# Softmax sums by row reductions instead of matmuls, in the first attention block of a four-block kernel

## The chip, the cores and the metric

The kernel runs on one core of one Trainium2 chip. The metric is the time on the device in microseconds (us). The core has five engines that run beside one another, each in the order of its own list of instructions: TensorE (PE; its weight loads are shown as PEld), VectorE (DVE), ScalarE (ACT), GpSimd (POOL) and SyncE (SP, which only issues DMAs here). They wait for each other through semaphores. PE writes to PSUM, which has 8 banks; DVE and ACT read the results from there.

## The reference

Four blocks follow one another on rows of 256 features. Only the first one is changed: a transformer block on x of shape (2, 2048, 256) with 16 query heads and 4 key heads of 16 features, a causal window of 64 keys, and a feed-forward part of 1024 features. Cut to what matters:

```python
h = layernorm(x, g1, b1)                       # applied to an already normalised x, see below
q, k, v = h @ Wq + bq, h @ Wk + bk, h @ Wv + bv
q, k = rope(q), rope(k)                        # 4 query heads share a key head
scores = q @ k.T / sqrt(16)
valid = (col <= row) & (row - col < 64)
attn = softmax(where(valid, scores, -1e9))     # exp(s - max) / sum(exp(s - max))
out = attn @ v
x = x + out @ Wo + bo
h2 = layernorm(x, g2, b2)
x = x + gelu(h2 @ Wf1 + bf1) @ Wf2 + bf2
```

Each block of the chain is preceded by a layer normalisation, so the kernel handles the first two normalisations of x together ("normalised twice" and "normalised once" in the code). After the first block come two layers of local attention with a gated feed-forward part, a gated attention block and a ternary linear layer. All data is float32.

## The kernel before, in words

**Tiles.** The 4096 rows of the first block are 32 tiles of 128 rows (the index t), in 8 groups of 4 tiles (the index g). A tile goes through a pipeline of four steps: in step t its queries, keys and values are computed, in step t+1 its scores, in step t+2 it attends, and in step t+3 the output projection is added. So a step works on four tiles at once, named in `step_a` p (project), q (scores), a (attend) and o (output). Layer normalisation and the feed-forward part (FFN) work on whole groups and are spread over the steps. Steps run from −5 to 35; the steps' numbers modulo 4 tell what a step holds besides its tiles: types 0 and 1 hold four of the eight FFN hidden products each (L555, two at each of two places in the step, `fill(0)` and `fill(1)`; each is two matmuls and one GELU, L561), types 2 and 3 hold FFN output products (L566, added by L573). Type 2 ends with the normalisation and transposes of the next group (`m`), type 3 with those of the FFN input (`f`).

**What a tile does, by line.** `project` (L383) makes a 128x384 product for queries, keys and values. `take` adds the bias (L392, DVE), copies the values to `vo` (L395, POOL) with one or two DMAs that shift half of the rows into `vmid`, and forms the two parts of the rotation: t2 on POOL (L406, L409), t1 on DVE (L414). `rotate` adds them (L419, L424, DVE) into a padded layout. `to_features` transposes that on PE (L430, L431), and ACT copies it out (L436, L437, L439). In the next step `scores` makes the products (L449) in 4 banks, `mask(g)` adds the mask for one key head (L459, DVE), `maxima(half)` takes row maxima over 128 keys for 8 heads (L468, DVE) and subtracts them (L469, POOL), and `exponents` (L472, ACT) takes the exponential of all 16 heads. In the step after that, `weights_to_keys` transposes the weights on PE (L479) and ACT copies them out (L487). `values` multiplies them with the values (L499), and once more with a matrix of ones (`one48`, L506), which gives each softmax sum, repeated over the 16 features of its head, in the second half of the same bank. `take_values` takes its reciprocal (L515, DVE, 128x256 elements from PSUM) and multiplies (L516). `output` (L521) and its addition to the residual (L527, DVE) come a step later.

**Normalisation.** The statistics are made on DVE and POOL (L145, L146, L162 or L135 and L137). `normalised_twice` (L169) and `normalised` (L197) apply them to four tiles on DVE; `normalised_once` (L178, L183) does it on ACT for the residual rows. `transposed` (L214 on PE, L219 on ACT) brings the result into features. `add_rows` (L206, POOL) adds biases and residuals.

**Order.** The lists of PE, DVE, ACT and POOL are in the order in which `step_a` calls these functions (the program is scheduled by hand); the SP queue's DMAs are ordered by a scheduler. Tiles of SBUF come from pools with a tag and a number of buffers, PSUM banks from one pool of 8. The call order within a step before the change is: scores, masks 0 and 1, project, take, mask 2, rotate, maxima 0, mask 3, maxima 1; fill 0; statistics; to_features; weights_to_keys and take_weights (ahead of to_features in steps without FFN work); fill 1; normalise; values and take_values; output and add_output; exponents; the groups' transposes; bias.

Of the kernel before, what the change touches and what calls it, by code (L numbers as in the profile page):

```python
# [17 lines left out]
P = 128  # L18
# [3 lines left out]
GT = 4  # L22
# [23 lines left out]
def kernel(ctx: ExitStack, tc: tile.TileContext, I: dict, out: bass.AP):  # L46
# [118 lines left out]
    def normalised_twice(src, stats, dst):  # L165

        mv, rs = stats
        for t in range(GT):
            nc.vector.tensor_scalar(  # L169
                dst[:, t, :], src[:, t, :], mv[:, t, 0:1], rs[:, 1, t : t + 1], ALU.subtract, ALU.mult  # L170
            )

    def normalised_once(src, stats, dst, residual):

        mv, rs = stats
        scale = rs[:, 0, :]
        shift = T(small, [P, GT], "sh2")
        nc.vector.scalar_tensor_tensor(shift, mv[:, :, 0], -1.0, scale, ALU.mult, ALU.mult)  # L178
        if residual:
            scale = T(small, [P, GT], "sc2")  # L180
            nc.vector.tensor_scalar_add(scale, rs[:, 0, :], 1.0)
        for t in range(GT):
            nc.scalar.activation(  # L183
                dst[:, t, :], src[:, t, :], AF.Identity,
                bias=shift[:, t : t + 1], scale=scale[:, t : t + 1],
            )
# [91 lines left out]
    class GroupA:  # L278
# [9 lines left out]

        def normalise(self):
            self.h = T(wa, [P, GT, D], "h", 1)  # L290
            normalised_twice(self.xg, self.stats, self.h)

        def residual(self):
            self.y = T(wa, [P, GT, D], f"y{self.g % 3}", 1)
# [74 lines left out]
    nc.gpsimd.memset(one48, 0.0)  # L369
    nc.gpsimd.memset(one48[:, AHD : 2 * AHD], 1.0)  # L370

    class TileA:


        def __init__(self, t, grp):
            self.t, self.grp = t, grp
            self.first = t % TPS == 0

        def project(self):
            hT, tt = self.grp.hT, self.t % GT  # L380
# [8 lines left out]
        def take(self):  # L389
            t, tl = self.t, self.t % TPS  # L390
            qkv = self.qkv = T(wa, [P, 384], "qkv")
            nc.vector.tensor_add(qkv, self.pm[:, :384], bqkvA)  # L392

            vo = vown[t % NVW]
            nc.gpsimd.tensor_copy(  # L395
                vo[:, :, AHD : 2 * AHD], qkv[:, 320:384].rearrange("p (g d) -> p g d", d=AHD)
            )
            load(vmid[t % NVW][64:128], vo[0:64])
            if tl < TPS - 1:
                load(vmid[(t + 1) % NVW][0:64], vo[64:128])  # L400

            nh, hf = AH + AKV, AHD // 2
            qk = self.qk = qkv[:, 0:320].rearrange("p (h d) -> p h d", d=AHD)
            sin = ropeA[:, tl, 1, :].unsqueeze(1)
            t2 = self.t2 = T(wa, [P, nh, AHD], "t2")
            nc.gpsimd.tensor_mul(  # L406
                t2[:, :, 0:hf], qk[:, :, hf:AHD], sin[:, :, 0:hf].to_broadcast([P, nh, hf])
            )
            nc.gpsimd.tensor_mul(  # L409
                t2[:, :, hf:AHD], qk[:, :, 0:hf], sin[:, :, hf:AHD].to_broadcast([P, nh, hf])  # L410
            )
            cos = ropeA[:, tl, 0, :].unsqueeze(1)
            self.t1 = T(wa, [P, nh, AHD], "t1", 1)
            nc.vector.tensor_mul(self.t1, qk, cos.to_broadcast([P, nh, AHD]))  # L414

        def rotate(self):
            nh, t1, t2 = AH + AKV, self.t1, self.t2
# [53 lines left out]
        def exponents(self):  # L471
            nc.scalar.activation(self.S, self.S, AF.Exp, scale=1.0 / AHD**0.5)  # L472

        def weights_to_keys(self):
            self.pts = []
            for g in range(AKV):
                pt = bank4()
                for c in range(AG):
                    nc.tensor.transpose(pt[:, c, :], self.S[:, g * AG + c, :], ident)  # L479
                self.pts.append(pt)  # L480
# [9 lines left out]
        def values(self):  # L490

            pm = self.po = bank().rearrange("p (s k q) -> p s k q", s=2, k=2)
            vw = (vmid[self.t % NVW], vown[self.t % NVW])
            for b in range(2):
                q = slice(64 * b, 64 * b + 64)
                for e in range(2):
                    c0 = 0 if e else AHD
                    for g in range(AKV):
                        nc.tensor.matmul(  # L499
                            pm[32 * g : 32 * g + 32, 0, :, q], vw[b][:, g, c0 : c0 + 32],  # L500
                            self.PT[g // 2][:, g % 2, :, e, q], start=e == 0, stop=e == 1,
                        )
            for e in range(2):
                c0 = 0 if e else AHD
                for g in range(AKV):
                    nc.tensor.matmul(  # L506
                        pm[32 * g : 32 * g + 32, 1, :, :], one48[:, c0 : c0 + 32],
                        self.PT[g // 2][:, g % 2, :, e, :], start=e == 0, stop=e == 1,
                    )

        def take_values(self):
            pm = self.po
            self.oT = T(wa, [P, KC, P], "oT")
            rd = T(wa, [P, KC, P], "rdA", 1)
            nc.vector.reciprocal(rd, pm[:, 1])  # L515
            nc.vector.tensor_mul(self.oT, pm[:, 0], rd)  # L516

        def output(self):
            pm = self.pm = bank()
# [9 lines left out]
    class FfnA:  # L529
# [9 lines left out]

        def normalise(self):  # L540
            self.h = T(wa, [P, GT, D], "h", 1)
            normalised(self.y, self.stats, self.h)
            add_rows(self.y, lambda t: bf2)

            add_rows(self.xr, lambda t: self.y[:, t, :])
# [43 lines left out]
        steps.setdefault(step, {}).setdefault(what, []).append(args)  # L589

    for t in range(NT):
        at(t, "project", t)
        at(t + 1, "scores", t)
        at(t + 2, "attend", t)
        at(t + 3, "output", t)
# [19 lines left out]
    def step_a(todo):  # L615
        p = a = q = o = n = m = f = e = None
        for (g,) in todo.get("load", ()):
            if g:
                groups_a[g] = GroupA(g)
        if "project" in todo:  # L620
            (t,) = todo["project"][0]
            if t == GT:
                weights.update({**load_qkv(0), **load_wo(0), **load_ffn(0)})
            p = tiles_a[t] = TileA(t, groups_a[t // GT])
        if "scores" in todo:
            q = tiles_a[todo["scores"][0][0]]
        if "attend" in todo:
            a = tiles_a[todo["attend"][0][0]]
        if "output" in todo:
            o = tiles_a.pop(todo["output"][0][0])  # L630
        for (g,) in todo.get("residual", ()):
            ffns_a[g] = FfnA(groups_a[g])
        if "statistics" in todo:
            n = groups_a[todo["statistics"][0][0]]
        if "normalise" in todo:
            m = groups_a[todo["normalise"][0][0]]
        if "prepare" in todo:
            f = ffns_a[todo["prepare"][0][0]]
        if "finish" in todo:
            e = ffns_a.pop(todo["finish"][0][0])  # L640

        def fill(place):

            rest = []
            for g, what, i in todo.get(f"fill{place}", ()):
                x = ffns_a[g]
                if what == "hidden":
                    rest.append(lambda x=x, i=i, r=x.hidden(i): x.take_hidden(i, r))
                else:
                    rest.append(lambda x=x, i=i, r=x.output(i): x.take_output(i, r))  # L650
            return rest

        if q:
            q.scores()
            q.mask(0)
            q.mask(1)
        if p:
            p.project()
            p.take()
        if q:  # L660
            q.mask(2)
        if p:
            p.rotate()
        if q:
            q.maxima(0)
            q.mask(3)
            q.maxima(1)
        pieces = fill(0)
        if a and not pieces:
            a.weights_to_keys()  # L670
            a.take_weights()
        for r in pieces:
            r()
        if n:
            n.statistics()
        if f:
            f.statistics()
        if e:
            e.last_statistics()
        if p:  # L680
            p.to_features()
            p.take_features()
        if a and pieces:
            a.weights_to_keys()
            a.take_weights()
        for r in fill(1):
            r()
        if m:
            m.normalise()
        if f:  # L690
            f.normalise()
        if e:
            e.last_normalise()
        if a:
            a.values()
            a.take_values()
        if o:
            o.output()
            o.add_output()
        if q:  # L700
            q.exponents()
        if m:
            m.to_features()
            m.residual()
        if f:
            f.to_features()
        for (g,) in todo.get("bias", ()):
            groups_a[g].add_bias()

# [1013 lines left out]
```

## Time and profile before

| | us |
|---|---|
| time, median of 3 runs | 2645.26 (2644.18 to 2648.4) |
| profiled execution, its own time | 2644.28 |
| its span in the profile | 2642.5 |
| first block, start to about | 500 |

The profile is of one execution. Busy times are sums for an engine or a group of instructions, "idle before" is what the engine waited just ahead of the group and for whom. Of the first block, these groups matter here (all from the groups by line for the first 680 us; xcount is the number of instructions):

| line, engine | what | xcount | mean ns |
|---|---|---|---|
| L506 PE | ones times weights, the sums | 512 | 387 |
| L499 PE | values times weights | 1024 | 283 |
| L430 PE | transposes of queries | 128 | 284 |
| L515 DVE | reciprocal of the sums, 128x256 | 32 | 1752 |
| L468 DVE | row maxima, 128x1024 | 64 | 1215 |
| L459 DVE | masks, 128x512 | 128 | 681 |
| L197 DVE | normalise FFN rows | 32 | 614 |
| L169 DVE | normalise rows of a group | 32 | 505 |
| L183 ACT | normalise residual rows | 32 | 592 |
| L561 ACT | GELU, 128x512 | 64 | 688 |

Each of these float32 matmuls stands in the trace as two records, so xcount and the chain's counts are twice the number of calls. Matmuls are pipelined, so the mean of one is longer than the time from one to the next: the chain of waits, which counts only the time by which each moves the end, is the better source for what a group of matmuls costs.

### The profile page before, as it was taken

The page shows a single profiled execution, that of the slowest core. Times are in us where ns is not written, and L with a number is a line of the kernel's source. Part 1 is how long each engine was busy: PE and PEld are TensorE (multiplying, and loading weights), DVE is VectorE, ACT ScalarE, POOL GpSimd, SP SyncE. Part 2 cuts the span into 40 slices and gives each one's busy share as a digit, 9 for nine tenths or more (in the row PEclk, how much of TensorE's full clock was granted, in tenths as well). Part 3 has the DMA queues.
Part 4 walks back from the last instruction along what each step waited for, and adds up shares of the span by engine and source line. Part 5 has one row for each costly group of instructions (what it writes and reads, how often), then busy time and mean ns, then how long its engine had stood idle before and what let it go on. Part 6 is the DMA issues. An engine that isn't in the chain of part 4 may idle for free.

```text
span 2642.5 us, 51312 instructions
## 1 busy us (share of the span) xinstructions
PE 2576.2 (97%) x20130; PEld 1645.9 (62%) x20130; DVE 1608.4 (61%) x4357; ACT 1199.7 (45%) x2507; POOL 995.4 (38%) x1237
## 2 busy tenths in 40 slices
PE   6899999998999999999999999999999999999998
PEld 4577777666666666666676676666544455445567
DVE  6878777567666766667666667774434335434344
ACT  3555555465666666756567666663500001500000
POOL 5565555545434544435444445542200002300011
PEclk8999999999999999999999999999999999999999
DMA  5001101111001011011310111101100000100000
GB/s 171 17 31 32 32 32 40 47 33 51 25 17 26 25 26 29 22 55 29 89 37 18 29 34 37 25 22 53 40 8 4 6 7 12 44 0 6 5 11 13
DMA packets 73169, 82.03 MB, mean 31 GB/s; under 512 B 18829, under 2 KB 57056, under 8 KB 72672
## 3 DMA queue, kind: packets, MB, share of 16 engines
q1 hardware_dynamic: 72928, 78.75, 10.6%
q8 instruction: 160, 2.62, 0.4%
q14 instruction: 81, 0.66, 0.1%
HBM read 44.20 MB, written 10.50 MB: 21 GB/s over the span
## 4 chain that ended last, share of the span: by engine, by line
PE 91%; DVE 4%; POOL 3%; issue 1%; DMA 0%; ACT 0%; SPq 0%; POOLq 0%; ACTq 0%; DVEq 0%
PE ps L1576 17%; PE ps L900 12%; PE ps L1154 10%; PE ps L1177 6%; PE ps L1500 4%; PE ps L566 4%; PE ps L555 4%; PE ps L1082 4%; PE ps L975 3%; PE ps L1053 2%; PE ps L1519 2%; PE ps L1488 2%; PE ps L1025 2%; PE ps L956 2%; PE ps L1478 2%; PE ps L479 2%
## 5 line engine op out<-in xcount | busy, mean ns | idle before, releaser
L1576 PE MATMUL ps<-room 128*128 128x512 f32 (+1 forms) x1152 | 463.2, 544 | 0.0
L1576 PEld LDWEIGHTS ps<-room 128*128 128x128 f32 x1152 | 217.8, 189 | 221.9 <-issue 214.7
L900 PE MATMUL ps<-room 128*128 128x512 f32 x768 | 347.4, 602 | 0.0
L1006 ACT ACTIVATE room<-room,shift,rn 128x192 f32<-128x192 f32 x512 | 276.0, 546 | 71.7 <-DVE shift L994 71.7
L921 POOL TENSOR_TENSOR room<-room 128x256 f32<-128x256 f32 x128 | 113.5, 887 | 500.6 <-ACT room L912 500.6
L1154 PE MATMUL ps<-room 128*128 128x512 f32 x640 | 287.6, 593 | 0.4 <-ACT room L219 0.4
L1544 ACT COPY room<-ps 128x256 f32<-128x256 f32 x32 | 11.8, 370 | 587.7 <-PE ps L1542 587.7
L939 POOL TENSOR_TENSOR rn<-ss,mhalf 128x8 f32<-128x8 f32 x128 | 248.2, 1939 | 10.7
L900 PEld LDWEIGHTS ps<-room 128*128 128x128 f32 x768 | 141.0, 190 | 157.8 <-issue 149.9
L1506 DVE SCALAR_TENSOR_TENSOR room<-ps,room 128x512 f32<-128x512 f32 (+1 forms) x144 | 90.1, 626 | 206.5 <-PE ps L1500 206.5
L1154 PEld LDWEIGHTS ps<-room 128*128 128x128 f32 x640 | 118.8, 190 | 137.3 <-issue 131.5
L1529 POOL TENSOR_SCALAR veC<-mvC 128x1 f32<-128x1 f32 x32 | 7.2, 224 | 453.2 <-DVE mvC L1527 453.2
L1177 PE MATMUL ps<-room 128*128 128x256 f32 x768 | 173.0, 379 | 0.0
L987 DVE CUSTOM_DVE_ANT_0 room<-ps,room 128x192 f32<-128x192 f32 x512 | 152.2, 353 | 14.7 <-PE ps L975 14.3
L1177 PEld LDWEIGHTS ps<-room 128*128 128x128 f32 x768 | 143.7, 190 | 24.8 <-issue 6.2
L1017 DVE TENSOR_SCALAR room<-room,rdB 128x192 f32<-128x192 f32 x512 | 151.7, 360 | 4.5
L1170 DVE SCALAR_TENSOR_TENSOR room<-ps,room 128x512 f32<-128x512 f32 x96 | 72.1, 751 | 125.6 <-PE ps L1154 86.8
L469 POOL TENSOR_TENSOR room<-room,mxA 128x1024 f32<-128x1024 f32 x64 | 120.2, 1898 | 58.5 <-PE ps L431 45.4
L936 DVE TENSOR_REDUCE ss<-room 128x8 f32<-128x512 f32 x128 | 81.9, 681 | 94.9 <-ACT room L914 94.9
L1500 PE MATMUL ps<-room 128*128 128x512 f32 (+1 forms) x288 | 133.4, 545 | 0.0
L219 ACT ACTIVATE room<-ps,room 128x512 f32<-128x512 f32 x80 | 58.1, 772 | 143.3 <-PE ps L214 143.0
L1082 PE MATMUL ps<-room 128*128 128x256 f32 x512 | 121.0, 379 | 0.0
(182 smaller groups left out, 5050.1 us busy)
## 6 DMA issues: line engine op xcount, KB each, us to landing
room<-room SPq DMA_DIRECT2D x144, 128.0 KB
room<-in_L_attn_x_dram SPq DMA_DIRECT2D x16, 512.0 KB
room<-in_rope_b_dram SPq DMA_DIRECT2D x16, 512.0 KB
xs<-room SPq DMA_DIRECT2D x8, 512.0 KB
room<-xs SPq DMA_DIRECT2D x8, 512.0 KB
room<-in_rope_c_dram SPq DMA_DIRECT2D x8, 512.0 KB
out_dram<-R SPq DMA_DIRECT2D x32, 128.0 KB
room<-in_L_ffn_w_dram SPq DMA_DIRECT2D x6, 640.0 KB
```

The lines of the kernel that those rows point to most:

```text
L469: nc.gpsimd.tensor_sub(Sh, Sh, mc.unsqueeze(2).to_broadcast([P, 2 * AG, P]))
L900: nc.tensor.matmul(pm, src[:, cols], self.w["wqkv"][:, k, part * BIN : (part + 1) * BIN], start=k == 0, stop=k == 1,)
L921: nc.gpsimd.tensor_mul(u2[:, :, 0:hd2], x[:, :, hd2:BHD], sin[:, :, 0:hd2].to_broadcast([P, BH, hd2]))
L939: nc.gpsimd.tensor_tensor(self.rn[part], ss, mhalf[:, 0:BH], ALU.pow)
L987: nc.vector.tensor_tensor_reduce(S[:, e, jj, :], sc[e][:, jj * KW : (jj + 1) * KW], self.mask[:, jj, :], 1.0, -3.0e38, ALU.add, ALU.max, t ...
L1006: nc.scalar.activation(S[:, e, jj, :], S[:, e, jj, :], AF.Exp, bias=self.shift[half][:, a : a + 1], scale=self.rn[0][:, head : head + 1], ...
L1017: nc.vector.tensor_scalar_mul(S[:, e, jj, :], S[:, e, jj, :], rd[:, a : a + 1])
L1082: nc.tensor.matmul(pm[:, 0:D], self.oT[:, k, :], wo[:, k, :], start=k == 0, stop=k == BIN // P - 1)
L1154: nc.tensor.matmul(pm, w["w1"][:, k, half, c * P : (c + 1) * P], hT[:, k, :], start=k == 0, stop=k == KC - 1,)
L1177: nc.tensor.matmul(pm[:, 0:D], hh[:, c, tt * P : (tt + 1) * P], self.w["w2"][:, c, :], start=c == 0, stop=c == BNC - 1,)
L1500: nc.tensor.matmul(pm[:, 0:n], self.KT[:, J * P : (J + 1) * P], self.QT[:, q0 : q0 + n], start=True, stop=True,)
L1576: nc.tensor.matmul(acc[e][:, 0:n], self.V[:, J, e * P : (e + 1) * P], s2, start=J == 0, stop=J == TPS - 1,)
```

## The change

It has four parts.

1. From tile 6 on (`by_features` is false), the matmuls with ones (L506) and the large reciprocal (L515) are left out. In their place, `sum_weights` at the very end of the attending step takes row sums of the exponentials on DVE (two reductions of 128x1024) and the reciprocal of the 16 sums of a row. At the next step, `spread_sums` on ACT repeats each reciprocal over 16 features, `sums_to_features` transposes this on PE (two transposes) and copies it out on ACT, and `take_values` multiplies (so it comes a step later than before, just ahead of the output projection's place in the order).
2. Tiles 1 to 6 are projected one step earlier; their `take` and `rotate` come ahead of the masks and maxima (`p.t < RAMP`).
3. For group 1's first normalisation and group 0's FFN normalisation, four ACT instructions take the place of four DVE instructions (`normalised_on_scalar`).
4. In `take`, the two t2 products on POOL and t1 on DVE come ahead of the value copy and its DMAs; t2 has one buffer instead of two.

The diff, cut to its core:

```diff
+    def normalised_on_scalar(src, mean, scale, dst):
+        shift = T(small, [P, GT], "sh2")
+        nc.vector.scalar_tensor_tensor(shift, mean, -1.0, scale, ALU.mult, ALU.mult)
+        for t in range(GT):
+            nc.scalar.activation(
+                dst[:, t, :], src[:, t, :], AF.Identity,
+                bias=shift[:, t : t + 1], scale=scale[:, t : t + 1],
+            )
...
         def normalise(self):                       # GroupA; FfnA alike with self.g == 0
-            normalised_twice(self.xg, self.stats, self.h)
+            if self.g == 1:
+                mv, rs = self.stats
+                normalised_on_scalar(self.xg, mv[:, :, 0], rs[:, 1, :], self.h)
+            else:
+                normalised_twice(self.xg, self.stats, self.h)
...
+    RAMP = 7
...
+            self.by_features = t < RAMP - 1
...
+        def sum_weights(self):
+            sums = T(wa, [P, AKV * AG], "sumsA", 1)
+            for half in range(2):
+                heads = slice(half * 2 * AG, (half + 1) * 2 * AG)
+                nc.vector.reduce_sum(sums[:, heads], self.S[:, heads, :], axis=AX.X)
+            self.rd = T(wa, [P, AKV * AG], "rdA", 1)
+            nc.vector.reciprocal(
+                self.rd.rearrange("p (k g e) -> p g k e", g=AKV, k=2),
+                sums.rearrange("p (g k e) -> p g k e", g=AKV, k=2),
+            )
+        def spread_sums(self):
+            self.rx = T(wa, [P, AKV * AG, AHD], "rx", 1)
+            nc.scalar.copy(self.rx, self.rd.unsqueeze(2).to_broadcast([P, AKV * AG, AHD]))
+        def sums_to_features(self):
+            pt = bank4()
+            for k in range(2):
+                nc.tensor.transpose(pt[:, k, :], self.rx[:, 2 * AG * k : 2 * AG * (k + 1), :], ident)
+            self.rT = T(wa, [P, KC, P], "rT", 1)
+            nc.scalar.copy(self.rT, pt[:, 0:KC, :])
...
-            for e in range(2):
+            for e in range(2) if self.by_features else ():
                 c0 = 0 if e else AHD
                 for g in range(AKV):
                     nc.tensor.matmul(                      # one48, L506
...
-            rd = T(wa, [P, KC, P], "rdA", 1)
-            nc.vector.reciprocal(rd, pm[:, 1])
-            nc.vector.tensor_mul(self.oT, pm[:, 0], rd)
+            if self.by_features:
+                self.rT = T(wa, [P, KC, P], "rT", 1)
+                nc.vector.reciprocal(self.rT, pm[:, 1])
+            nc.vector.tensor_mul(self.oT, pm[:, 0], self.rT)
...
-        at(t, "project", t)
+        at(t - 1 if 0 < t < RAMP else t, "project", t)
+        at(t, "take", t)
...
         if q:
             q.scores()
-            q.mask(0)
-            q.mask(1)
-        if p:
-            p.project()
+        for (t,) in todo.get("project", ()):
+            tiles_a[t].project()
+        if p and p.t < RAMP:
             p.take()
+            if q:
+                q.mask(0)
+                q.mask(1)
+            p.rotate()
+            if q:
+                q.maxima(0)
+                q.mask(2)
+        else:
+            ...                                   # the order before, with project ahead of mask(0)
...
+        if o and not o.by_features:
+            o.spread_sums()
         if p:
             p.to_features()
             p.take_features()
+        if o and not o.by_features:
+            o.sums_to_features()
+            o.take_values()
...
         if a:
             a.values()
-            a.take_values()
+            if a.by_features:
+                a.take_values()
         if o:
             o.output()
             o.add_output()
...
         if f:
             f.to_features()
+        if a and not a.by_features:
+            a.sum_weights()
```

More of the change, by code (lines that the diff above doesn't have):

```diff
@@ L392, in take @@
             nc.vector.tensor_add(qkv, self.pm[:, :384], bqkvA)
[L394 to L400, printed above, removed]
             nh, hf = AH + AKV, AHD // 2
@@ L404, in take @@
             sin = ropeA[:, tl, 1, :].unsqueeze(1)
-            t2 = self.t2 = T(wa, [P, nh, AHD], "t2")
+            t2 = self.t2 = T(wa, [P, nh, AHD], "t2", 1)
             nc.gpsimd.tensor_mul(
@@ L414, in take @@
             nc.vector.tensor_mul(self.t1, qk, cos.to_broadcast([P, nh, AHD]))
+            vo = vown[t % NVW]
+            nc.gpsimd.tensor_copy(
+                vo[:, :, AHD : 2 * AHD], qkv[:, 320:384].rearrange("p (g d) -> p g d", d=AHD)
+            )
+            load(vmid[t % NVW][64:128], vo[0:64])
+            if tl < TPS - 1:
+                load(vmid[(t + 1) % NVW][0:64], vo[64:128])
         def rotate(self):
@@ L472, in exponents @@
             nc.scalar.activation(self.S, self.S, AF.Exp, scale=1.0 / AHD**0.5)
+        def sum_weights(self):
[7 more added lines that the diff above has]
+                sums.rearrange("p (g k e) -> p g k e", g=AKV, k=2),
+            )
+        def spread_sums(self):
[7 more added lines that the diff above has]
+            nc.scalar.copy(self.rT, pt[:, 0:KC, :])
         def weights_to_keys(self):
@@ L541, in normalise @@
             self.h = T(wa, [P, GT, D], "h", 1)
-            normalised(self.y, self.stats, self.h)
+            if self.g == 0:
+                mv, rs = self.stats
+                normalised_on_scalar(self.y, mv[:, :, 0], rs, self.h)
+            else:
+                normalised(self.y, self.stats, self.h)
             add_rows(self.y, lambda t: bf2)
@@ L619, in step_a @@
                 groups_a[g] = GroupA(g)
-        if "project" in todo:
-            (t,) = todo["project"][0]
+        for (t,) in todo.get("project", ()):
             if t == GT:
                 weights.update({**load_qkv(0), **load_wo(0), **load_ffn(0)})
-            p = tiles_a[t] = TileA(t, groups_a[t // GT])
+            tiles_a[t] = TileA(t, groups_a[t // GT])
+        if "take" in todo:
+            p = tiles_a[todo["take"][0][0]]
         if "scores" in todo:
@@ L654, in step_a @@
             q.scores()
-            q.mask(0)
-            q.mask(1)
-        if p:
-            p.project()
+        for (t,) in todo.get("project", ()):
+            tiles_a[t].project()
+        if p and p.t < RAMP:
             p.take()
-        if q:
[L661 to L665, printed above, removed]
+            if q:
[5 more added lines that the diff above has]
+                q.mask(2)
+        else:
+            if q:
+                q.mask(0)
+                q.mask(1)
+            if p:
+                p.take()
+            if q:
+                q.mask(2)
+            if p:
+                p.rotate()
+            if q:
+                q.maxima(0)
+        if q:
             q.mask(3)
```

## The prediction

> **What bounds the kernel now.** I read the page's shares, its slices, the windows of the first block, the chain of waits in a steady stretch, then single instructions around the edit. On the page:
>
> ```profile
> PE 2576.2 (97%) x20130; PEld 1645.9 (62%) x20130; DVE 1608.4 (61%) x4357; ACT 1199.7 (45%) x2507; POOL 995.4 (38%) x1237
> ```
>
> PE is busy for 97% of the span, so only what shortens PE's own list, or an idle stretch of PE, can move the end. The windows (columns PE, PEld, DVE, ACT, POOL busy, clock, DMA) show where such stretches are in the first block:
>
> ```profile
> 40.00:60.00 20.00, 16.74 (x274) 11.84 (x275) 19.22 (x29) 10.78 (x18) 9.90 (x10) 0.91 0.80 226
> ...
> 260.00:340.00 80.00, 80.00 (x875) 59.52 (x874) 62.17 (x123) 42.35 (x66) 40.83 (x46) 1.00 0.11 34
> ```
>
> Until about 105 us DVE is nearly full (19.22 of 20 us) and PE waits for it; from 120 to 500 us PE has no gap. One steady step, as the chain of waits has it (start, length):
>
> ```profile
> 302.82 1.06 PE ps L521 x4
> 303.89 1.14 PE ps L449 x63
> 305.02 1.49 PE ps L383 x4
> 306.51 3.43 PE ps L555 x8
> 309.94 0.44 PE ps L430 x4
> 310.38 0.11 PE ps L431
> 310.49 1.75 PE ps L479 x16
> 312.24 3.44 PE ps L555 x8
> 315.67 1.01 PE ps L499 x32
> 316.68 0.86 PE ps L506 x16
> 317.55 1.06 PE ps L521 x4
> ```
>
> The step is 14.72 us (L521 to L521); steps with the second FFN product (L566) and one L214 are 15.64 us apart on average. L506 is what the change removes. From the starts in the timeline (316.50 for L506, 317.48 for L521, with the overlap of neighbouring groups that the chain cuts off) it holds PE for 0.97 us.
>
> **The change, part by part.**
>
> *Sums on PE.* 26 tiles (6 to 31) lose L506: 26 × 0.97 = 25.2 us. They gain two transposes at L430's rate (0.44/4 = 0.11 us each): 26 × 0.22 = 5.7 us. Gross: −19.5 us, −0.75 per tile, if nothing waits.
>
> *Sums on DVE.* The groups (busy, mean ns):
>
> ```profile
> L468 DVE TENSOR_REDUCE mxA<-room 128x8 f32<-128x1024 f32 x64 | 77.8, 1215 | 1.1
> ...
> L515 DVE RECIPROCAL room<-ps 128x256 f32<-128x256 f32 x32 | 56.1, 1752 | 39.4 <-PE ps L506 39.4
> ...
> L1544 ACT COPY room<-ps 128x256 f32<-128x256 f32 x32 | 11.8, 370 | 587.7 <-PE ps L1542 587.7
> ```
>
> Two row sums of L468's shape stand against one L515. [...] By the rows here, a sum costs 1.215 us for 1024 elements, and the reciprocal 1.752 us for 256. A sum of this shape isn't in the trace, but the second block has one of 512 elements (L936, 681 ns), so it lies between 1.215 (L468's maximum of the same shape) and 1.36 (two of L936); I take L468's, 1.13 from start to start. The reciprocal of 16 numbers lies between L1014 (168 ns for 4) and half of L515; I take 0.24. So DVE goes from 1.75 to 2.5 us per tile. [...] By the rows DVE goes from 62.2 to about 62.2 + 5 × 0.75 = 66 of 80 us, so it isn't full and PE keeps the saving, less what the place costs: the 2.5 us stand at the end of a step, ahead of the next tile's masks.
>
> *Waits that this makes,* each per step (types are the step's number modulo 4):
> - Steps of type 2 (FFN product, no L214 before them). With P the start of L383: the residual sum L527 runs at P−1.02, the row sums and reciprocal fill DVE to P+1.85, where the masks L459 used to start at P+0.41. Two masks bring L392 to P+3.04, the rotation L419 to P+4.69 (t2 now precedes the copy L395 on POOL, else 0.45 later), L430 to P+5.26. PE gets there at P+4.85 (319.67 to 324.52 in the trace). Wait 0.41, plus 0.13 in the later weight transposes for the fourth mask's bank: 0.54.
> - Types 0 and 1 (hidden products L555). ACT's new copy of the reciprocals (bounds L437's 275 and L436's 585 ns; L1544's 0.37 taken, same size) stands behind the step's second GELU:
>
> ```profile
> 295.06 0.60 PE L430 MATMUL ps<-ident,room 128*128 128x128 f32 x4
> ...
> 295.26 0.69 ACT L561 ACTIVATE room<-ps,room 128x512 f32<-128x512 f32 x1 [1.03 <-PE ps L555]
> ...
> 295.85 0.58 ACT L436 COPY room<-ps 128x512 f32<-128x512 f32 x1
> ```
>
>  That GELU starts 0.20 after L430; 0.59 later the copy, 0.37 later its end, with hand-over 1.21 after L430's start. PE wants it 0.55 after: 0.66 us of wait. L436 to L439, the new rT copy (0.37) and L487 queue behind it on ACT; L499, which needs L487, has 2.3 us in hand (282.97 against 285.29), so nothing more is lost. The rotation's lateness of 0.41 passes inside the 0.66.
> - Type 3 (f.normalise, L197): PE arrives at its L214 0.97 earlier. In the trace L197 runs from 285.84 to 288.05 and L214 starts at 288.13; the first three transposes need only the first three rows, so they can precede the last row by 3 × 0.11, and L214 can come 0.40 earlier, not 0.97. Wait 0.57.
>
> Net per step −0.09, −0.09, −0.21, −0.18: −0.57 per four. Steps 9 to 31: 23/4 × 0.57 = −3.3 us. Step 8 has no transposes yet: −0.97. Steps 32 to 34 have no feature transposes between GELU and sum transposes, so PE meets the wait whole (1.21): +0.46, +0.46, and +0.22 in step 34: +1.1.
>
> If waits of this size lowered PE's clock, they'd cost far more; from 60 to 80 us PE had 1.82 us of idle in small pieces and the granted clock was 1.00, so I charge nothing.
>
> *The ramp* (0 to 105 us). Projection a step ahead frees L392 from PE, but in step 1 DVE waits for group 1's x, landing at 31.47, and in step 2 for POOL, whose rs and bias rows (L162, L206) hold the rotation until 39.7, nearly as before (39.93). Rows on ACT take L169 (2.95 us) off DVE, and put 4 × 0.515 us on ACT ahead of the exponentials L472 and the copies L219, so that project(4), now in step 3, waits for L219 until about 49.4: the reciprocal of step 3 comes at +0.2. Steps 4 and 5 then win 0.5 each, the masks no longer waiting for L383; the FFN rows of group 0 on ACT end near 103.8 instead of 104.66. I take −0.95 (bounds: −4, L169 and part of L197's 2.2 kept whole; +3, ACT's two row blocks in PE's way).
>
> *At nothing:* L395 and two vmid DMAs moved behind t2 on POOL and SP (1.03 us later; their reader L499 is two steps away, 25 us; without that cover 1.0 per step); t2 with one buffer (its reader is the same step's L419); L516 moved (same 0.42); the output bank held a step longer (seven of eight banks are otherwise free in turn; the one wait found is the 0.13).
>
> Sum: −3.3 − 0.97 + 1.1 − 0.95 = −4.1 us. The profiled execution is 2644.28 us, 1.0 under the median of 2645.26; the median becomes 2641.2.
>
> **Rivals.**
> - *The waits are mostly absent.* For it: DVE has slack inside a step (2.95 us idle before L515 at 317.62), and PE's arrival times could shift by more than the waits. Then −19.5 − 1 ≈ 2625; half of the waits gone, 2633. Against: gelu order and DVE order are fixed, and the times above come from starts in the trace.
> - *DVE's lateness binds (slower).* Place: masks and rotation behind the row sums. Each 0.1 us more there delays L430 in about three of four steps: 23 × 0.75 × 0.1 = 1.7 us. From 0.25 us per tile on (a row sum of 1.34 instead of 1.215) the 4.1 are gone; at 0.55 (1.49 each) it's +9.5 − 4.1, 2650.7. For it: the 1.85 us shift is larger than any slack before L430. Against: L468 varies little.
> - *ACT rows delay the ramp:* +3 instead of −0.95, 2645.
>
> **How the numbers follow.** About 0.2% (5.3 us) is what a measurement of this kernel tells from no change, and the forecast's −4.1 lies just inside. The forecast with its own bounds (−10 to 0, so 2635 to 2645): 48%, of it 0.20 beyond −5.3. Waits absent: 21%, all faster. DVE binds: 24%, of it 0.20 past +5.3. Ramp: 7%, of it 0.02 past +5.3. So faster 0.20 + 0.21 = 0.41, slower 0.20 + 0.02 = 0.22, same the remaining 0.37. Range: the forecast, most of the first rival (to 2630) and of the second (to 2651).
>
> **What would show it.** Right: in the profile after, from 120 to 490 us PE idles about 14 us, waiting at the first sum transpose for the ACT copy by 0.6 to 0.7 in steps with L555 and at L430 for DVE by 0.4 in others; L506 has 96 entries left; step pitch 14.6. Wrong: PE without gaps (first rival), or gaps above 1 us before L430 (second). A clock under 1.00 in those windows, or a ramp that ends more than 3 us off 105, would also break the sum.

## The result, and the profile after

The changed kernel is slower: 2655.24 us (median of 6 runs, 2652.62 to 2656.69) against 2644.5 us (6 runs of the kernel before beside it), a ratio of 1.0037 with a 95% interval of 1.0024 to 1.005. I had forecast 2641.2 in a range of 2630 to 2651. The profiled execution took 2654.86 us, its span is 2653.1 against 2642.5.

Line numbers from here on are those of the changed kernel, where they have moved: scores L468, projection L402, bias L411, t2 L417 and L420, value copy L428, rotation L438 and L443, query transposes L449, masks L478, maxima L487, row sums L498, their reciprocal L501, its copy L508, sum transposes L513, weights' transposes L522, values L542, multiplication L561, output L566 and its addition L572, FFN products L604 (hidden, GELU L610) and L615 (output, addition L622), rows L207 and their transposes L224.

The page's shares after, then the steady window (columns as before: PE, PEld, DVE, ACT, POOL, clock):

```profile
PE 2569.6 (97%) x19766; PEld 1638.2 (62%) x19766; DVE 1620.1 (61%) x4403; ACT 1221.2 (46%) x2567; POOL 993.9 (37%) x1237
```

```profile
260.00:340.00 80.00, 77.49 (x838) 56.58 (x826) 65.31 (x130) 47.08 (x78) 40.26 (x45) 1.00 0.09 27
```

PE has less work, as intended, but is no longer full: 2.5 us in 80 are gaps, and the clock is still 1.00. DVE has risen from 62.17 to 65.31, close to the 66 of the prediction, and is far from full. The chain of waits after shows who makes the gaps in a step of type 2 (start, length):

```profile
319.95 1.07 PE ps L566 x4
...
321.05 0.42 DVE room L572
321.47 2.26 DVE room L498 x2
...
324.01 1.14 DVE room L478 x2
325.15 0.47 DVE room L411
...
325.76 0.07 POOL room L417
325.82 0.66 issue
326.49 0.52 POOL room L420
...
327.04 0.44 DVE room L438
...
327.52 0.66 PE ps L449 x4
```

Before, this chain ran on PE alone. Now it leaves PE after the output product and goes through DVE's row sums, two masks and bias and through POOL's t2 products to the rotation, before it comes back to PE 6.5 us later, at the query transposes. (Of L417's 0.76 us the chain shows 0.07 as its own and 0.66 as "issue".)

Taking the start of L449 (before) or L468 (after), the scores, as the start of a step, steps of one type agree within 0.02 us in both traces from step 9 to 29 (steps 30 and 31 differ, as the groups run out), so the account can be made step by step. In the lower five rows the forecast is the difference from before:

| | before | forecast | after |
|---|---|---|---|
| step of type 0 | 14.72 | 14.63 | 14.82 |
| step of type 1 | 14.72 | 14.63 | 15.03 |
| step of type 2 | 15.63 | 15.42 | 15.93 |
| step of type 3 | 15.63 | 15.45 | 15.73 |
| ramp, to the start of step 8 | 105.97 | −0.95 | 105.44 (−0.53) |
| step 8 | 15.72 | −0.97 | 15.97 (+0.25) |
| steps 9 to 31 | 348.68 | −3.3 | 354.11 (+5.43) |
| steps 32 to 34 | 32.99 | +1.1 | 35.20 (+2.21) |
| start of the first block's last FFN products | 503.35 | −4.1 | 510.72 (+7.37) |

So +7.37 us of the +10.6 us between the two spans arise in the first block. Another 1.5 us are added near 620 us, 0.45 more by 663 us, and 1.2 us in the last 7 us of the program, in code that the change doesn't touch. More on these below.

One of the prediction's own signs would have passed, and misled. It expected about 14 us of idle PE from 120 to 490 us, and the windows show 13.0 in the changed kernel:

```profile
120.00:490.00 370.00, 357.00 (x3732) 253.13 (x3725) 298.20 (x601) 219.02 (x352) 204.16 (x238) 1.00 0.10 32
```

But idle time starts only when the last matmul has drained. In the step of type 2 the transposes L449 start 0.59 us later than PE's list alone would have them, and the timeline gives 0.43 of that as idle. Counted by starts, PE waits about 20 us in steps 9 to 31.

### The profile page after: what moved, and what is told of

Same layout as the page of the kernel before. It is cut to its first block, busy times and chain, and to the rows that moved or that the text cites. A ratio compares the mean times of both kernels' runs of the same rounds, so it can differ in the third digit from the quotient of the medians.

```text
span 2653.1 us, 50755 instructions
## 1 busy us (share of the span) xinstructions
PE 2569.6 (97%) x19766; PEld 1638.2 (62%) x19766; DVE 1620.1 (61%) x4403; ACT 1221.2 (46%) x2567; POOL 993.9 (37%) x1237
## 4 chain that ended last, share of the span: by engine, by line
PE 82%; DVE 9%; POOL 4%; issue 3%; DMA 1%; ACT 1%; SPq 1%; POOLq 0%; ACTq 0%; DVEq 0%
PE ps L1649 16%; PE ps L973 12%; PE ps L1227 10%; PE ps L1250 6%; PE ps L1573 4%; PE ps L1155 4%; PE ps L1048 3%; PE ps L1126 2%; PE ps L604 2%; PE ps L1592 2%; PE ps L1561 2%; PE ps L1098 2%; PE ps L1029 2%; PE ps L1551 2%; PE ps L615 2%
## 5 line engine op out<-in xcount | busy, mean ns | idle before, releaser
L1649 PEld LDWEIGHTS ps<-room 128*128 128x128 f32 x1152 | 217.8, 189 | 221.9 <-issue 214.7
L973 PEld LDWEIGHTS ps<-room 128*128 128x128 f32 x768 | 141.0, 190 | 157.7 <-issue 150.2
L1227 PEld LDWEIGHTS ps<-room 128*128 128x128 f32 x640 | 118.8, 190 | 137.3 <-issue 131.8
L1250 PEld LDWEIGHTS ps<-room 128*128 128x128 f32 x768 | 143.7, 190 | 24.8 <-issue 6.5
L488 POOL TENSOR_TENSOR room<-room,mxA 128x1024 f32<-128x1024 f32 x64 | 120.3, 1896 | 58.8 <-DVE mxA L487 33.3
L1155 PEld LDWEIGHTS ps<-room 128*128 128x128 f32 x512 | 97.3, 190 | 34.1 <-issue 23.2
```

What stands on the lines that cost most here:

```text
L488: nc.gpsimd.tensor_sub(Sh, Sh, mc.unsqueeze(2).to_broadcast([P, 2 * AG, P]))
L973: nc.tensor.matmul(pm, src[:, cols], self.w["wqkv"][:, k, part * BIN : (part + 1) * BIN], start=k == 0, stop=k == 1,)
L1155: nc.tensor.matmul(pm[:, 0:D], self.oT[:, k, :], wo[:, k, :], start=k == 0, stop=k == BIN // P - 1)
L1227: nc.tensor.matmul(pm, w["w1"][:, k, half, c * P : (c + 1) * P], hT[:, k, :], start=k == 0, stop=k == KC - 1,)
L1250: nc.tensor.matmul(pm[:, 0:D], hh[:, c, tt * P : (tt + 1) * P], self.w["w2"][:, c, :], start=c == 0, stop=c == BNC - 1,)
L1649: nc.tensor.matmul(acc[e][:, 0:n], self.V[:, J, e * P : (e + 1) * P], s2, start=J == 0, stop=J == TPS - 1,)
```

## The experiments

Each runs beside the kernel before. The medians of the kernel before were 2646.79 us (41 runs) beside experiments 1 to 4 and 2647.54 us (9 runs) beside 5 to 8, against 2644.5 us beside the changed kernel, so kernels of different sets are compared by their ratio to it or by the lengths of their steps. Experiments 5 to 7 have one run each, and only their steps are used.

**1. The sums by matmuls again.** `self.by_features = True` for all tiles; the three other parts of the change stay.

> The changed kernel with the sums taken by matmuls with ones for all 32 tiles again; tiles projected a step ahead, rows normalised on ScalarE and the order in take stay. Theory (the loss is made by the new sums: DVE's row sums stand ahead of the next tile's masks, the copy of the reciprocals behind a GELU): the four steady steps are back at 14.72 + 14.72 + 15.63 + 15.64 = 60.7 us, the first block ends within 1 us of the kernel before, time 2643 to 2645. Rival (the loss comes from the ramp, the moved value copy or the blocks that follow): the time stays above 2650.

Measured: 2645.37 us, ratio 0.9996 (0.9988 to 1.0005), no difference. Steps last 14.72, 14.72, 15.63 and 15.63 us, as before the change, and the block's last FFN products start 0.98 us ahead of the kernel before. So the loss belongs to the new sums. The other three parts together bring nothing in the steady steps; of the 0.98 us, 0.76 are the ramp's and 0.19 step 8's, which is within what these two vary by (see below).

**2. The row sums moved on DVE.**

```diff
         if o and not o.by_features:
             o.sums_to_features()
             o.take_values()
+        if a and not a.by_features and not f:
+            a.sum_weights()
...
-        if a and not a.by_features:
+        if f and a and not a.by_features:
             a.sum_weights()
```

> The changed kernel with the row sums moved on DVE: ahead of the weights' transposes of the same step, right after the multiplication by the reciprocals, where DVE was idle for 1.3 to 2.8 us; only in the steps that normalise FFN rows they stay at the end. Theory (lateness of masks and rotation costs about 0.95 us in a step of type 1 and 0.9 in one of type 2): type 2 loses its wait (step 15.93 to about 15.05), type 1 exchanges its wait for the one behind the GELU (15.03 to about 14.8), so 6 x 0.9 + 6 x 0.2 = 6.6 us less than the changed kernel, near 2648.5. Rival (DVE's amount, not its place): no change, 2655.

Measured: 2645.24 us, ratio 0.9999 (0.9991 to 1.0007). Type 2 fell from 15.93 to 14.99, type 1 from 15.03 to 14.82, and type 3, where I had expected nothing, from 15.73 to 15.44. The row sums at the end of a step's list run in the next step, ahead of its masks, so moving those of a type 2 step relieves type 3. The amount of work on DVE is the same as in the changed kernel; only its place differs. The rival "amount" falls.

**3. The reciprocals' copy ahead of the GELUs.** `spread_sums` is called for tile a after `sum_weights`, at the end of the step, instead of for tile o ahead of `to_features`.

> The changed kernel with ScalarE's copy of the reciprocals moved to the end of the attending step, ahead of the next step's GELUs; row sums stay at the end of the step. Theory (this copy behind the second GELU costs 0.69 us in steps of type 0 and 1.07 + 1.46 in steps 32 and 33, and nothing in type 1, where the rotation is later still): 5 x 0.69 + 2.5 = 6 us less than the changed kernel, near 2649; type 0 steps 14.82 to 14.15, type 1 stays at 15.03. Rival (the copy's place does not matter because DVE's lateness takes its room): 2655.

Measured: 2649.13 us, ratio 1.0011 (1.0004 to 1.0017). Type 0 went from 14.82 to 14.08, the other three stayed within 0.01: 15.03, 15.93, 15.72. This is the 0.69 us of the GELU with 0.05 on top, in type 0 alone.

**4. Both moves.**

> Both moves together. Theory: types 0, 1 and 2 lose their new waits (0.69 + 0.95 + 0.9 us per four steps), type 3 keeps the 0.8 behind the FFN's normalised rows; 6 x 2.5 + 2.5 = 17.5 us less than the changed kernel, 2637 to 2638, which is 0.25% faster than the kernel before. Rival (something else takes over, such as the fourth mask's bank or ScalarE's list): above 2642.

Measured: 2634.05 us, ratio 0.9951 (0.9939 to 0.9964): faster than both kernels, and by more than expected, in part for the reason seen in experiment 2. Steps last 14.08, 14.08, 14.99 and 15.44 us, so that steps 9 to 31 take 12.1 us less than before (336.57 against 348.68), close to the 12.7 us between the medians. The waits of PE between 120 and 470 us, of the changed kernel (first fence) and of this one (second; columns: total, times, longest):

```profile
PE ps L449 <- DVE room L443: 3.2, 6, 0.5
PE ps L449 <- DVE room L438: 3.0, 7, 0.4
PE ps L513 <- ACT room L508: 2.6, 5, 0.5
PE ps L224 <- DVE room L207: 1.9, 5, 0.4
```

```profile
PE ps L224 <- DVE room L207: 1.4, 6, 0.2
```

The rotation (L438, L443) went with the first move, the copy (L508) with the second; what remains is the FFN's rows in type 3.

**5. What the matmuls with ones cost PE.** In the kernel before they are left out, and the reciprocal is taken of the first half of the bank, so the softmax is not normalised.

> The kernel before with the matmuls with ones left out for all tiles and nothing in their place (the reciprocal, of the same shape, is taken from the values instead, so the softmax is not normalised). It measures what leaving them out is worth to PE. By the prediction's term: 0.97 us per step in types 0 to 2 (13.75, 13.75, 14.67 us per step), and 0.40 in type 3 (15.23), because the FFN's normalised rows come no earlier. By the length in the chain of waits: 0.86 (13.86, 13.86, 14.77), type 3 as before.

Measured in one run (2631.15 us): steps of 13.86, 13.86, 14.77 and 15.34 us. So their absence is worth 0.86 in types 0 to 2, not 0.97. A step of type 3, in its chain (line numbers of the kernel before):

```profile
334.10 3.47 PE ps L566 x16
...
337.60 0.42 DVE room L573
...
338.05 2.21 DVE room L197 x4
...
340.31 0.76 PE ps L214 x5
```

With the ones gone, PE's FFN product, the addition L573 and four rows L197 are a chain of their own, and PE waits at its end. This step keeps 0.30 of the 0.86 (15.34 against 15.63).

**6. The value copy first again.** Part 4 is undone (t2 keeps one buffer).

> The changed kernel with the value copy and its DMAs ahead of the two t2 products in take again (t2 keeps its one buffer). Theory (POOL's products stand on the way to the rotation, which is late in types 1 and 2): the rotation comes 0.2 to 0.25 us later, types 1 and 2 last 15.25 and 16.15 us instead of 15.03 and 15.93, type 3 up to 0.1 more, type 0 the same; 12 x 0.22 = +2.6 us by the end of the first block. Rival (POOL's order is hidden): no change in any step.

Measured in one run (2659.83 us): 14.82, 15.23, 16.12 and 15.93: about +0.20 in types 1, 2 and 3, nothing in type 0. That is 3.5 us in steps 9 to 31. So the fourth part of the change is a gain where the rotation is late, of the size expected per step, and it reaches type 3 as well.

**7. A third row sum.**

```diff
+            again = T(wa, [P, 2 * AG], "againA", 1)
+            nc.vector.reduce_sum(again, self.S[:, 0 : 2 * AG, :], axis=AX.X)
```

> The changed kernel with a third row sum of 128x1024 on DVE at the end of each step (its result is not used). Theory (DVE's place at the step's end binds through the next masks and rotation): types 1 and 2 last 1.13 us longer (16.16, 17.06), type 3 about 1.0 longer because its rotation ends only 0.14 before PE arrives (16.7), type 0 about as before (14.9), because its 0.69 behind the GELU takes the lateness in; 5.75 x 3.3 = +19 us by the end of the first block. Rival (DVE has room in the step, 66 of 80 us busy): under +5 us.

Measured in one run (2677.51 us): types 0 to 3 last 15.17, 16.12, 17.01 and 16.82, so +0.35, +1.09, +1.08 and +1.09. Steps 9 to 31 grow by 21.4 us (375.53 against 354.11), 19 expected. A microsecond put in that place costs the block nearly a microsecond in three of four steps, though DVE was idle for 14.7 of 80 us in the changed kernel's window.

**8. Both moves, and the FFN's rows split over two engines.**

```diff
-                normalised(self.y, self.stats, self.h)
+                ...
+                for t in range(GT):
+                    if t % 2 == 0:
+                        nc.vector.tensor_scalar(
+                            self.h[:, t, :], self.y[:, t, :], mv[:, t, 0:1], rs[:, t : t + 1],
+                            ALU.subtract, ALU.mult,
+                        )
+                    else:
+                        nc.scalar.activation(
+                            self.h[:, t, :], self.y[:, t, :], AF.Identity,
+                            bias=shift[:, t : t + 1], scale=rs[:, t : t + 1],
+                        )
```

> Both moves of the row sums and the reciprocals' copy, and the FFN's normalised rows split: two of four on ScalarE, two on DVE, in every group but the first. Theory: what is left above PE's own list after the two moves is type 3 (15.44 against 14.99 in type 2), where the last normalised row holds the transposes; the split takes 1.1 us off that row, type 3 falls to about 15.0, 6 x 0.45 = 2.7 us less than with the two moves alone, 0.994 of the kernel before. Rival (the exponentials, which then stand behind the rows on ScalarE, come too late): type 3 stays at 15.4 or type 0 grows by as much.

Measured: 2634.74 us, ratio 0.9952 (0.9938 to 0.9965). Type 3 fell to 14.99 as expected (type 0 is 14.16 instead of 14.08), and PE is full again (columns as above):

```profile
260.00:340.00 80.00, 80.00 (x853) 60.85 (x852) 65.97 (x141) 50.09 (x85) 44.17 (x50) 1.00 0.12 40
```

Steps 9 to 31 are 2.3 us shorter than in experiment 4 (334.26 against 336.57), but the times of the two can't be told apart; the last section says what lies over them.

## Why the prediction was wrong

The direction was wrong because both sides of a small difference were mis-sized. The forecast booked a gain of 0.75 us per step on PE and set waits of 0.54 to 0.66 against it. The gain was smaller and all four waits were larger:

| per step, us | type 0 | type 1 | type 2 | type 3 |
|---|---|---|---|---|
| gain on PE, forecast | 0.75 | 0.75 | 0.75 | 0.75 |
| gain on PE, measured | 0.64 | 0.64 | 0.64 | 0.64 |
| wait, forecast | 0.66 | 0.66 | 0.54 | 0.57 |
| wait, measured | 0.74 | 0.95 | 0.94 | 0.74 |

The measured gain is what is left when the waits are gone: steps of 14.08, 14.08 and 14.99 us in experiment 4, and 14.99 for type 3 in experiment 8. The measured wait is what the changed kernel's step lasts beyond that. Over the 23 steps from 9 to 31 the gain is 2.5 us short and the waits are 5.6 us over, and step 31 waits 0.8 us more than its type, as no group is normalised ahead of it any more. With the −3.3 of the forecast this makes +5.6; measured are +5.4. The places were right in types 0, 2 and 3, and wrong in type 1.

*Sums on PE: the term 0.97.* It is 0.86 (experiment 5). I had taken the difference of the starts of L506 and L521, which holds the time until L506 has drained. But L499, when it is the last group ahead of L521, needs that time itself: it took 0.90 from its start to L506's, and takes 1.01 to L521's. The chain of waits, quoted in the prediction, had 0.86, and I chose the other number. That is 0.11 per step, 2.9 us in all. The two new transposes take the 0.22 forecast (0.86 less 0.64).

*Type 2: the term 0.54.* DVE's steps came as written. P, the start of L402, is 322.08 us in the step whose chain is shown above. The timeline has this of it (start, length, idle time before with its releaser):

```profile
325.65 0.49 DVE L425 TENSOR_TENSOR room<-room 128x320 f32<-128x320 f32 x1
325.76 0.76 POOL L417 TENSOR_TENSOR room<-room 128x160 f32<-128x160 f32 x1 [2.98 <-DVE room L411]
...
326.49 0.51 POOL L420 TENSOR_TENSOR room<-room 128x160 f32<-128x160 f32 x1
...
327.04 0.43 DVE L438 TENSOR_TENSOR room<-room 128x256 f32<-128x256 f32 x1 [0.29 <-POOL room L420]
...
327.52 0.66 PE L449 MATMUL ps<-ident,room 128*128 128x128 f32 x4 [0.43 <-DVE room L438]
```

The addition is at P−1.03 (forecast −1.02), the masks at P+1.85 in the timeline (+1.85), L411 at P+2.99 (+3.04). The rotation, though, is at P+4.96 and not at P+4.69. The step that failed is POOL's: I gave both t2 products the 0.52 us that they had before. As the first in POOL's list, L417 takes 0.76 here (782 ns on average over steps 9 to 31). Before, the value copy stood there, and that was what took 542 ns instead of the 233 that it takes behind the products. What POOL does first runs beside DVE's t1 product (L425, which starts 0.03 to 0.12 us ahead of it) and lasts 0.26 us (product) or 0.31 us (copy) longer on average; with the copy moved away, the product has the delay. Where L417 starts when t1 is done, at 39.16 and 80.86 us in the ramp, it takes 0.52; there it also follows straight on L216, so these two starts don't tell t1's part from that of the idle stretch ahead of it. The rest speaks for t1: L488, first after 1.7 us of idle, takes 1.90 us, as its second does; and over steps 9 to 31 L417 takes 0.76 or 0.77 us where it starts more than 0.1 us behind t1, and 0.82 or 0.83 where it starts within 0.05, so it ends about 0.87 us after t1's start each time. In the step shown the two overlap for 0.38 us, and the delay is 0.24. No experiment took the two apart. Experiment 6 gives the balance: the new order in `take` gains 0.20 in a step whose rotation is late, and I had booked 0.45. PE waits 0.59 at L449 (327.52 against 326.93), and 0.29 in L522 for the mask of the fourth bank (2.20 us instead of 1.91), 0.13 in the forecast.

*Types 0 and 1: the term 0.66.* Type 0 has the wait as forecast:

```profile
358.56 0.60 PE L449 MATMUL ps<-ident,room 128*128 128x128 f32 x4
358.76 0.69 ACT L610 ACTIVATE room<-ps,room 128x512 f32<-128x512 f32 x1 [1.03 <-PE ps L604]
...
359.34 0.39 ACT L508 COPY room<-room 128x256 f32<-128x256 f32 x1
...
359.79 0.44 PE L513 MATMUL ps<-ident,room 128*128 128x128 f32 x2 [0.53 <-ACT room L508]
```

L449 to L513 is 1.23 where 0.55 would do: 0.68. Type 1 does not. There the rotation is so late (L449 waits 0.70, from 311.88, where the FFN product leaves PE, to 312.58) that the GELU is long under way and the copy waits for nothing else, so the wait is the rotation's, and L522 has another 0.21 for the bank. "The rotation's lateness of 0.41 passes inside the 0.66" was thus the wrong way round, and 0.70 + 0.21 stand in place of 0.66:

```profile
312.58 0.63 PE L449 MATMUL ps<-ident,room 128*128 128x128 f32 x4 [0.54 <-DVE room L443]
```

*Type 3: the term 0.57.* The wait for the FFN's rows is where it was forecast, and there is a second one ahead of it:

```profile
343.61 2.04 PE L522 MATMUL ps<-ident,room 128*128 128x128 f32 x16
...
351.89 0.77 PE L224 MATMUL ps<-ident,room 128*128 128x128 f32 x5 [0.38 <-DVE room L207]
```

L522 takes 0.13 more than its 1.91, for the bank of the fourth mask, as in type 2; I had booked that in type 2 alone. From the start of L224 (351.02) to the next scores are 1.57 us where 0.97 would do: 0.60. With the row sums moved out of the step before (experiment 2), the 0.13 is gone and the 0.60 becomes 0.45. So the row sums' lateness reached the FFN's statistics and rows as well, which I had not followed.

*The rest.* Steps 32 to 34 came at +2.21 instead of +1.1: they measured +0.67, +1.03 and +0.53 where +0.46, +0.46 and +0.22 were taken, with waits of PE at L513 of 1.07 and 1.46 us in the first two and about 0.25 in the third. The ramp's −0.95 can't be judged: the seven traces whose kernels are alike up to step 8 (the changed kernel and experiments 1 to 4, 7 and 8) reach it between 104.99 and 106.25 us, and the kernel before, in one trace, at 105.97. Step 8 came at +0.25 instead of −0.97 because of PE's clock. In the changed kernel it was at half until 110.04 us, 4.6 us into the step, in the kernel before until 108.33, 2.4 us into it. Without that the steps would be near 13.86 (14.08 less two transposes) and 14.72, so the clock took 2.1 us of the one and 1.0 of the other. In experiments 6 and 7, with the same list on PE, step 8 took 14.48.

*Which rival it was.* "DVE's lateness binds" named the place, and its price of 1.7 us per 0.1 us is close to the 1.9 that experiment 7 gives (21.4 us for 1.13). It was to decide from 0.25 us of extra lateness per tile; the lateness of the rotation was 0.27, nearly all of it POOL's. By that price it is 4.6 us of the 8.7 by which steps 9 to 31 missed the forecast; no run has POOL's product at its old length, so this stays an estimate. What was wrong is what I looked at to weigh it: I held the row sum's duration to be the uncertain thing. It took 1.207 us against 1.215 assumed; the uncertain thing stood downstream of it.

*What lies outside the steps.* The spans differ by 10.6 us, the first block by 7.37, of which 1.1 are the clock's in step 8. The other 3.2 us are the clock's too: 1.5 where the changed kernel had half the clock from 622.0 to 625.5 us and the kernel before had none near there; 0.45 where both restart at half the clock (652.8 to 663.0 and 644.2 to 654.5); and 1.2 at the end, where the changed kernel's last matmuls run at half the clock from 2646.1 us on, while it fell behind the last matmul of the kernel before (2641.0). So some 4.3 of the 10.6 us in these two traces are restarts. What stays open is whether the changed kernel meets them at a worse point more often: of the other five runs behind its median there is no trace.

## What to carry to other kernels

Before work is moved from a full engine to one with idle time, ask what is queued behind its new place, and follow that to the full engine: at the step's end, 2.5 us of row sums cost 0.95 and 0.94 us in types 1 and 2, more than the 0.86 of the matmuls that they replaced, and 4 to 6 us earlier, behind the multiplication L561, they cost nothing there. Take the worth of a removed group from the length by which it moved the chain's end, not from the starts around it, and a wait from the starts, not from the idle time. An edit that was made for a saving on one engine may only need its instructions placed again: experiment 4 has the whole of the change, in another order, and is 0.49% faster than the kernel before.

## What the runs showed of the hardware

*The clock after a gap.* The first group's FFN rows leave PE idle for 3.4 to 3.8 us, until about 103 us, in these kernels, and it restarts at half its clock (0.50 from 104 to 106 us, in the changed kernel and in the one before). (The waits of up to 0.7 us in the steady steps left it at 1.00.) How long that lasts isn't settled by the kernel's lists: windows of 2 us, of the changed kernel (first) and of the kernel with a third row sum (second), whose lists are alike up to there:

```profile
106.00:108.00 2.00, 2.00 (x57) 1.55 (x42) 0.42 (x1) 1.98 (x3) 2.00 (x4) 0.50 0.00 0
108.00:110.00 2.00, 2.00 (x4) 1.01 (x3) 0.87 (x2) 0.56 (x1) 0.42 (x2) 0.50 0.00 0
110.00:112.00 2.00, 2.00 (x6) 0.95 (x5) 1.65 (x3) 0.00 (x1) 1.08 (x2) 0.99 0.00 0
```

```profile
106.00:108.00 2.00, 2.00 (x66) 1.69 (x53) 0.35 (x1) 1.98 (x4) 2.00 (x4) 0.70 0.00 0
108.00:110.00 2.00, 2.00 (x7) 1.00 (x6) 1.88 (x4) 0.80 (x1) 1.00 (x3) 1.00 0.00 0
```

In the one the granted clock is at half from 103.2 to 110.0 us, in the other from 103.8 to 107.2. The step is 1.5 us longer for it (15.97 against 14.48). So half clock lasted 6.8 us in the one trace and 3.4 us in the other; what decides between the two, no run shows. Such restarts come again from about 520 us, where the blocks join (mean granted clock from 520 to 540 us: 0.83 in the kernel before and in the changed one), and near 620 to 660 us (from 640 to 660: 0.74 and 0.82, in the same order). Experiment 8 shows what this hides: in its trace it is 0.6 us ahead of experiment 4's when step 31 ends (2.3 us gained in the steady steps, less 0.74 in the ramp and 0.97 in step 8), and 4.75 us behind by 663 us: between 500 and 663 us its clock was at half for 27.3 us, in the other trace for 13.7 (mean granted clock of the two whole executions: 0.987 and 0.990). This is enough to hide a gain of 2.3 us in the kernel's time. So a difference in one stage is better read from the lengths of its steps, which repeat to 0.02 us in this kernel, than from the end of the kernel.

*Reductions and reciprocals on DVE.* A row sum of 128x1024 took 1.207 us (1.2 ns per element of a row) and the reciprocal of 128x256 from PSUM 1.752 us (6.8). Two reciprocals from SBUF, of 4 elements at 168 ns and of 16 at 253, differ by 7 ns per element. So the reduction is the cheaper of the two by far. The new sums and their reciprocal still fill DVE for 2.5 us instead of 1.75, as forecast.
